# Causal attention on one core: no maximum pass, four row tiles for the scores, key sums on VectorE, a written order

## The chip, the core and the metric

The kernel runs on one core of a Trainium2 chip. The metric is the device time of one execution in microseconds, here written us. The core has five engines that work side by side, each through its own instructions in order: TensorE (PE in the profile; its weight loads are PEld), VectorE (DVE), ScalarE (ACT), GpSimd (POOL) and SyncE (SP), which only issues transfers here. All data are float32.

## The reference, cut to what matters

```python
# x: (32, 256, 32, 32), standard normal; q_w (256, 256), kv_w (512, 256) scaled by 1/16
xf = gn(x).reshape(B, C, S)                 # 32 groups of 8 channels; S = 1024
q = einsum('oc,bcs->bos', q_w, xf) + q_b
kv = einsum('oc,bcs->bos', kv_w, xf) + kv_b
k, v = kv[:, :256], kv[:, 256:]             # 8 heads of 32 channels
mask = tril(ones((S, S)), -1)               # a query sees earlier keys only, not itself
scores = where(mask == 0, -10000.0, q @ k.T / sqrt(32))
attn = where(mask == 0, 0.0, softmax(scores, axis=-1))
return x + attn @ v
```

Query 0 sees no key, so its attention is zero and its output is x. For every other query a hidden key adds exp(-10000 - largest) to the sum, which counts only where the largest visible score is near -10000.

## The kernel before, in words

The 256 channels lie on partitions in two chunks `g` of 128, four heads in each. Each of the 32 batches goes through two phases, and the first phase of a batch is interleaved with the second phase of the one before it.

The first phase normalises (`norm_channels`, `norm_mean`, `norm_apply`, L157 to L193), projects Q and K with channels on partitions (`project_qk`, L202, copied out by ScalarE at L206) and V with keys on partitions (`project_v`, L227, bias added by VectorE at L232). The maximum pass is `largest` (L247): for each block of 128 queries and each head a score product with queries on partitions, whose row maximum VectorE takes (L252, and L255 for the block with the diagonal). A head has 32 rows, so a product uses 32 of the 128 rows of the array. `shift_rows` (L268 to L282) turns the maxima into rows by a transpose and moves them by DMA into a 33rd row beside Q. For this, Q and K are also copied by DMA (L216) into tiles where the heads of a pair start at partitions 0 and 64.

The second phase takes, for each chunk, each half `hf` of 512 queries and each block `k` of 128 keys that the half sees, a step: `weights` computes the scores again with keys on partitions (L305), with 33 rows, two heads at a time; VectorE adds the mask to diagonal blocks (L311), ScalarE takes the exponential of two heads at once (L313). `values` (L332) multiplies the exponentials with V, four heads in four column tiles of 32, and a second time with a matrix of ones, which gives each query's sum of exponentials, copied to the 32 partitions of its head. `pick` (L323) starts the sums with what the hidden keys add. After the last key block ScalarE copies the accumulator out (L341), VectorE takes the reciprocal of 512 columns (L342) and multiplies (L343), GpSimd adds x (L348) and SP issues the output (L350).

A batch has 24 steps: per chunk four for the first half (512, 384, 256 and 128 queries see the key block) and eight for the second (five of 512, then 384, 256, 128). The order is that in which the program is written, one step behind for `values`, with the units of the next batch's first phase dealt out evenly over the steps (L369 to L387); the scheduler may still exchange instructions of an engine where dependencies allow it.

```python
for n in range(2):                       # values: V, then ones
    for j in range(4):
        jj, par = divmod(j, 2)
        nc.tensor.matmul(
            acc[HD * j : HD * (j + 1), n, c0:],
            lhsT=ones if n else live["v", b][:, k, h * HD : (h + 1) * HD],
            rhs=tiles[jj][:, par, c0:], ...)
```

Of the kernel before, what the change touches and what calls it, by code (L numbers as in the profile page):

```python
# [9 lines left out]
F32 = mybir.dt.float32  # L10
# [3 lines left out]
AX = mybir.AxisListType  # L14
PSUM = bass.MemoryType.PSUM
# [6 lines left out]
LOWEST = -1.0e30  # L22


@with_exitstack
def tile_norm_attention_residual(
# [25 lines left out]
    NB = S // P  # L52
    SCALE = 1.0 / math.sqrt(HD)

    const = ctx.enter_context(tc.tile_pool(name="const", bufs=1))
    xpool = ctx.enter_context(tc.tile_pool(name="xpool", bufs=3))
    npool = ctx.enter_context(tc.tile_pool(name="npool", bufs=2))
    apool = ctx.enter_context(tc.tile_pool(name="apool", bufs=3))
    vpool = ctx.enter_context(tc.tile_pool(name="vpool", bufs=2))
    epool = ctx.enter_context(tc.tile_pool(name="epool", bufs=6))  # L60
    opool = ctx.enter_context(tc.tile_pool(name="opool", bufs=2))
    small = ctx.enter_context(tc.tile_pool(name="small", bufs=3))
    ps_a = ctx.enter_context(tc.tile_pool(name="ps_a", bufs=2, space=PSUM))
    ps_s = ctx.enter_context(tc.tile_pool(name="ps_s", bufs=2, space=PSUM))
    ps_o = ctx.enter_context(tc.tile_pool(name="ps_o", bufs=1, space=PSUM))

    def bank(name):
        return ps_a.tile([P, HALF], F32, tag="bank", name=name)

# [4 lines left out]
    ident = const.tile([P, P], F32, name="ident")  # L74
    make_identity(nc, ident)
    ones = const.tile([P, HD], F32, name="ones")
    nc.gpsimd.memset(ones, 1.0)
    masked_bias = const.tile([P, 1], F32, name="masked_bias")
    nc.gpsimd.memset(masked_bias, MASKED)
# [3 lines left out]
    # Added to scores whose last 128 columns are a diagonal block [query, key].  # L83
    mask = const.tile([P, HALF], F32, name="mask")
    nc.gpsimd.memset(mask, 0.0)
    nc.gpsimd.affine_select(
        out=mask[:, HALF - P :], in_=mask[:, HALF - P :], pattern=[[-1, P]],
        compare_op=ALU.is_gt, fill=LOWEST, base=0, channel_multiplier=1,
    )
    # The same for a pair of heads' diagonal blocks [key, query].  # L90
    mask_t = const.tile([P, 2, P], F32, name="mask_t")
    nc.gpsimd.memset(mask_t, 0.0)
    nc.gpsimd.affine_select(
        out=mask_t, in_=mask_t, pattern=[[0, 2], [1, P]],
        compare_op=ALU.is_gt, fill=LOWEST, base=0, channel_multiplier=-1,
    )
# [46 lines left out]
    for n in range(3):  # L143
        t = const.tile([P, 2, S], F32, name=f"k_pair_{n}")
        for par in range(2):
            nc.gpsimd.memset(t[64 * par + HD : 64 * par + HD + 1, :, :], 1.0)
# [267 lines left out]
```

## Time and profile before

| | |
|---|---|
| timed runs | 7592.06, 7596.24 (median), 7607.42 us |
| span of the profiled execution, first to last instruction | 7550.2 us |
| other time of the profiled execution | not given on the page |
| instructions | 67242 |
| PE / DVE / ACT / POOL busy | 94% / 39% / 20% / 3% |
| mean granted TensorE clock | 0.737 |
| DMA, share of 16 engines | 6.5% |

A busy share counts time in which at least one instruction of the engine runs. Matmuls are pipelined and their ends are modelled, so rows of one engine can overlap, and the time of a group of products is read from its start to the start of the next. A granted clock of 1.00 is 2.4 GHz, 0.50 is 1.2 GHz.

### The profile page before, as it was taken

The numbers are of one execution on the slowest core, as the hardware profiler recorded it, in microseconds if no ns is written. First come the engines' busy times: TensorE is split into PE (matmuls) and PEld (weight loads), VectorE is DVE, ScalarE is ACT, GpSimd is POOL, SyncE is SP. The second block draws the span as 40 slices with busy tenths as digits, with TensorE's granted clock in tenths as the row PEclk, the third lists the DMA queues.
The fourth block names the chain that finished last, engine by engine and source line by source line (L and its number), as shares of the span: only waits on it lengthen the run. The fifth ranks groups of instructions, "written<-read, shape, count | busy, mean of one in ns | idle before, by whom it ended". The sixth has DMA issues, their size and how long they took to land. (4 is left out here: it accounts for less than half of the span.)

```text
span 7550.2 us, 67242 instructions
## 1 busy us (share of the span) xinstructions
PE 7074.5 (94%) x27084; PEld 2446.2 (32%) x27084; DVE 2918.8 (39%) x7272; ACT 1512.2 (20%) x1985; POOL 199.6 (3%) x185
## 2 busy tenths in 40 slices
PE   8999999999999999999999999999999999999999
PEld 3333333333333333333333333333333333333333
DVE  4333333343343334333333333333343334334433
ACT  0111212112122122221211212121121211212213
POOL 0000000000000000000000000000000000000000
PEclk6767777777677768777777767777776777777778
DMA  1000000000000000000000000000000000000000
GB/s 35 13 23 15 23 11 21 23 15 23 9 23 23 15 23 19 13 23 15 23 15 17 23 15 23 9 23 23 15 23 11 21 23 15 23 19 14 23 12 15
DMA packets 50713, 141.59 MB, mean 19 GB/s; under 512 B 12640, under 2 KB 17632, under 8 KB 50400
## 3 DMA queue, kind: packets, MB, share of 16 engines
q1 hardware_dynamic: 50400, 137.28, 6.5%
q8 instruction: 213, 3.49, 0.2%
q14 instruction: 100, 0.82, 0.0%
HBM read 34.47 MB, written 33.55 MB: 9 GB/s over the span
## 5 line engine op out<-in xcount | busy, mean ns | idle before, releaser
L247 PE MATMUL sc<-k,q 32*128 32x512 f32 (+3 forms) x6144 | 2606.8, 719 | 419.6 <-DVE far L252 245.0
L313 ACT ACTIVATE e<-sT 128x1024 f32<-128x1024 f32 (+3 forms) x1536 | 1195.3, 809 | 5208.2 <-DVE sT L311 3900.3
L247 PEld LDWEIGHTS sc<-k,q 32*128 32x128 f32 x6144 | 902.2, 235 | 2262.4 <-DVE top L255 939.4
L305 PE MATMUL sT<-q_pair,k_pair 33*128 33x512 f32 (+3 forms) x6144 | 1588.9, 614 | 2.1 <-ACT e L313 0.8
L332 PE MATMUL acc<-e,v 128*32 128x512 f32 (+3 forms) x6144 | 1374.6, 664 | 0.0
L332 PE MATMUL acc<-e,ones 128*32 128x512 f32 (+3 forms) x6144 | 1355.5, 656 | 0.0
L305 PEld LDWEIGHTS sT<-q_pair,k_pair 33*128 33x128 f32 x6144 | 642.0, 225 | 1036.0 <-issue 933.7
L252 DVE TENSOR_REDUCE far<-sc 128x1 f32<-128x512 f32 x1024 | 680.4, 688 | 635.6 <-PE sc L247 635.6
L255 DVE CUSTOM_DVE_ANT_0 junk<-sc,mask,far 128x128 f32<-128x128 f32 (+3 forms) x1024 | 560.5, 550 | 918.5 <-PE sc L247 917.0
L255 DVE CUSTOM_DVE_ANT_0 junk<-sc,mask 128x128 f32<-128x128 f32 (+3 forms) x1024 | 473.2, 485 | 1104.8 <-PE sc L247 1104.6
L311 DVE TENSOR_TENSOR sT<-sT,mask_t 128x256 f32<-128x256 f32 x1024 | 430.1, 429 | 1125.4 <-PE sT L305 1005.4
L342 DVE RECIPROCAL acc_sb<-acc_sb 128x512 f32<-128x512 f32 x128 | 429.1, 3352 | 301.5 <-ACT acc_sb L341 301.5
L202 PE MATMUL pp<-xn,wT 128*128 128x512 f32 x1024 | 542.5, 679 | 1.0 <-DVE xn L190 1.0
L332 PEld LDWEIGHTS acc<-e,ones 128*32 128x32 f32 x6144 | 286.5, 135 | 465.0 <-issue 446.0
L332 PEld LDWEIGHTS acc<-e,v 128*32 128x32 f32 x6144 | 192.7, 122 | 746.8 <-issue 712.4
L348 POOL TENSOR_TENSOR y<-acc_sb,x 128x512 f32<-128x512 f32 x128 | 162.2, 1267 | 6758.2 <-DVE acc_sb L343 5663.0
L202 PEld LDWEIGHTS pp<-xn,wT 128*128 128x128 f32 x1024 | 213.3, 219 | 303.0 <-issue 267.4
L227 PE MATMUL ppv<-wT,xn 128*128 128x256 f32 x1024 | 242.5, 385 | 22.9 <-DVE v L232 22.9
L227 PEld LDWEIGHTS ppv<-wT,xn 128*128 128x128 f32 x1024 | 189.5, 190 | 75.6 <-DVE v L232 28.5
L255 DVE DVE_READ_ACCUMULATOR2_ANT top<- 128x1 f32 x2048 | 170.3, 83 | 0.0
L341 ACT COPY acc_sb<-acc 128x1024 f32<-128x1024 f32 x128 | 129.6, 1012 | 194.9 <-PE acc L332 194.8
L323 PE MATMUL acc<-extra,pick 4*128 4x512 f32 x256 | 168.4, 742 | 0.0
(50 smaller groups left out, 811.4 us busy)
## 6 DMA issues: line engine op xcount, KB each, us to landing
x<-in_x_dram SPq DMA_DIRECT2D x32, 1024.0 KB
q_pair<-q SPq DMA_DIRECT2D x256, 128.0 KB
k_pair<-k SPq DMA_DIRECT2D x256, 128.0 KB
out_dram<-y SPq DMA_DIRECT2D x64, 512.0 KB
q_pair<-rows SPq DMA_DIRECT2D x128, 8.0 KB
extra<-rows SPq DMA_DIRECT2D x64, 16.0 KB
wn<-in_L_conv_kv_w_dram SPq DMA_DIRECT2D x2, 256.0 KB
wn<-in_L_conv_q_w_dram SPq DMA_DIRECT2D x1, 256.0 KB
```

What stands on the lines that cost most here:

```text
L202: nc.tensor.matmul(pp, lhsT=wT[:, cc, n * C + g * P : n * C + (g + 1) * P], rhs=xn[:, cc, hf * HALF : (hf + 1) * HALF], start=cc == 0, sto ...
L227: nc.tensor.matmul(pp[:, s, :], lhsT=xn[:, cc, (2 * n + s) * P : (2 * n + s + 1) * P], rhs=wT[:, cc, 2 * C : 3 * C], start=cc == 0, stop=c ...
L247: nc.tensor.matmul(sc[:, : k1 - k0], lhsT=q[rows, i * P : (i + 1) * P], rhs=k[rows, k0:k1], start=True, stop=True,)
L252: nc.vector.tensor_reduce(far[:, r, i : i + 1], sc[:, : k1 - k0], AX.X, ALU.max)
L255: nc.vector.tensor_tensor_reduce(out=junk[:, : k1 - k0], in0=sc[:, : k1 - k0], in1=mask[:, HALF - (k1 - k0) :], scale=1.0, scalar=far[:, r ...
L305: nc.tensor.matmul(sc[:, par, c0:], lhsT=k2[rows, jj, k * P : (k + 1) * P], rhs=q2[rows, jj, hf * HALF + c0 : (hf + 1) * HALF], start=True ...
L311: nc.vector.tensor_add(diagonal, diagonal, mask_t)
L313: nc.scalar.activation(e[:, :, c0:], sc[:, :, c0:], AF.Exp)
L323: nc.tensor.matmul(live["acc"][:, 1, :], lhsT=pick, rhs=live["extra", b, g][:, hf * HALF : (hf + 1) * HALF], start=True, stop=False, skip_ ...
L332: nc.tensor.matmul(acc[HD * j : HD * (j + 1), n, c0:], lhsT=ones if n else live["v", b][:, k, h * HD : (h + 1) * HD], rhs=tiles[jj][:, par ...
L342: nc.vector.reciprocal(both[:, 1, :], both[:, 1, :])
L348: nc.gpsimd.tensor_add(y[:, cols], both[:, 0, :], live["x", b][:, g, cols])
```

## The change

The kernel gets two functions. `unshifted` computes everything with exponentials of the plain scores; it keeps track of whether every sum of exponentials lies within 1e-20 and 1e20. `shifted` computes everything with the maximum subtracted, in a loop over the batches, and stands behind a branch on that record.

In `unshifted` the maximum pass, `shift_rows`, the 33rd row, the DMA copies of Q and K and the products with ones are gone. A score step takes its four heads from partitions 0, 32, 64 and 96 of Q and K as projected, in four row tiles, into four banks. The diagonal block is masked after the exponential, by GpSimd. The sums of exponentials are first added over key blocks by VectorE (into the tile of the first key block), and only then over partitions by one product per head; the four (chunk, half) results of a batch share one tile `den`. Their reciprocal is taken once per batch in four pieces, spread to the heads' partitions by 16 DMAs, multiplied and added to x some steps into the next batch. `values` runs two steps behind `scores`. On PE, ACT, DVE and POOL the instructions stay in the order in which they are written.

PSUM before: 2 single banks, 2 pairs for scores, a pair as accumulator. After: 3 pairs for scores, 1 bank as accumulator, 1 bank for all else.

```diff
-            for par in range(2):
-                rows = slice(64 * par, 64 * par + HD + 1)
-                nc.tensor.matmul(
-                    sc[:, par, c0:], lhsT=k2[rows, jj, k * P : (k + 1) * P],
-                    rhs=q2[rows, jj, hf * HALF + c0 : (hf + 1) * HALF], start=True, stop=True,
-                )
-            if k * P >= hf * HALF:
-                diagonal = sc[:, :, c0 : c0 + P]
-                nc.vector.tensor_add(diagonal, diagonal, mask_t)
...
+        def scores(b, g, hf, k):
+            q, kk = live["q", b, g], live["k", b, g]
+            c0 = max(k * P - hf * HALF, 0)
+            tag = "e0" if k == 0 else "e"
+            e = epool.tile([P, 4, HALF], F32, tag=tag, bufs=2 if k == 0 else None, name=f"{tag}_{b}_{g}_{hf}_{k}")
+            pairs = [ps_s.tile([P, 2, HALF], F32, tag="sT", name=f"sT_{b}_{g}_{hf}_{k}_{a}") for a in range(2)]
+            for j in range(4):
+                rows = slice(HD * j, HD * (j + 1))
+                nc.tensor.matmul(
+                    pairs[j // 2][:, j % 2, c0:], lhsT=kk[rows, k * P : (k + 1) * P],
+                    rhs=q[rows, hf * HALF + c0 : (hf + 1) * HALF], start=True, stop=True,
+                )
+            for a in range(2):
+                nc.scalar.activation(e[:, 2 * a : 2 * a + 2, c0:], pairs[a][:, :, c0:], AF.Exp)
+            if k * P >= hf * HALF:
+                diagonal = e[:, :, c0 : c0 + P]
+                nc.gpsimd.affine_select(
+                    out=diagonal, in_=diagonal, pattern=[[0, 4], [1, P]],
+                    compare_op=ALU.is_gt, fill=0.0, base=0, channel_multiplier=-1,
+                )
+                if k == 0:
+                    nc.gpsimd.memset(e[0:1, :, 0:1], 1.0)
...
+        def values(b, g, hf, k):
...
+            for j in range(4):
+                h = 4 * g + j
+                nc.tensor.matmul(
+                    acc[HD * j : HD * (j + 1), c0:], lhsT=live["v", b][:, k, h * HD : (h + 1) * HD],
+                    rhs=e[:, j, c0:], start=k == 0, stop=k == last, skip_group_check=True,
+                )
+            if k:
+                nc.vector.tensor_add(total[:, :, c0:], total[:, :, c0:], e[:, :, c0:])
+            if k == last:
...
+                nc.scalar.copy(live["num", b][:, g, hf * HALF : (hf + 1) * HALF], acc)
+        def sums(b, g, hf):
+            n = NH * g + hf
+            total = live.pop(("sum", b, g, hf))
+            pd = misc(f"pd_{b}_{n}")
+            for j in range(4):
+                nc.tensor.matmul(
+                    pd[HD * j : HD * (j + 1), :], lhsT=pick[:, n, :], rhs=total[:, j, :],
+                    start=True, stop=True, skip_group_check=True,
+                )
+            if n == 0:
+                live["den", b] = small.tile([P, HALF], F32, tag="den", name=f"den_{b}")
+                nc.vector.tensor_copy(live["den", b], pd)
+            else:
+                nc.vector.tensor_add(live["den", b], live["den", b], pd)
+        def check_sums(b):
+            den = live["den", b]
+            nc.vector.scalar_tensor_tensor(in_range, den, SUM_MIN, in_range, ALU.is_ge, ALU.mult)
+            nc.vector.scalar_tensor_tensor(in_range, den, SUM_MAX, in_range, ALU.is_le, ALU.mult)
+        def invert(b, c):
...
+            cols = slice(c * P, (c + 1) * P)
+            nc.vector.reciprocal(live["rec", b][:, cols], live["den", b][:, cols])
+        def spread(b):
...
+                    nc.sync.dma_start(
+                        out=rb[HD * j : HD * (j + 1), n // NH, (n % NH) * HALF : (n % NH + 1) * HALF],
+                        in_=src.unsqueeze(1).broadcast_to([1, HD, HALF]),
+                    )
+        def finish(b, n):
...
+            nc.vector.tensor_mul(rb[:, g, cols], num[:, g, cols], rb[:, g, cols])
+            nc.gpsimd.tensor_add(rb[:, g, cols], rb[:, g, cols], xt[:, g, cols])
...
+        for b in range(B):
+            if b + 2 < B:
+                when(b * N, lambda b=b: load(b + 2))
+                for n, f in zip((4, 6, 10, 14, 16, 18), prepare(b + 2)):
+                    when(b * N + n, f)
+            if b + 1 < B:
+                for n, f in enumerate(projections(b + 1)):
+                    when(b * N + 2 * n + 1, f)
+            for s, (g, hf, k) in enumerate(per):
+                if k == (hf + 1) * BPH - 1:
+                    when(b * N + s + LAG + 2 + (s + LAG) % 2, lambda b=b, g=g, hf=hf: sums(b, g, hf))
+            end = (b + 1) * N + LAG + 2
+            when(end, lambda b=b: check_sums(b))
+            for c in range(BPH):
+                when(end + 1 + c, lambda b=b, c=c: invert(b, c))
+            when(end + BPH, lambda b=b: spread(b))
+            for n in range(4):
+                when(end + BPH + 5 + n, lambda b=b, n=n: finish(b, n))
+        with tc.manual_schedule(engines={ENG.PE, ENG.Activation, ENG.DVE, ENG.Pool}):
...
+            for i in range(max(max(at), len(steps) + LAG) + 1):
+                if i < len(steps):
+                    scores(*steps[i])
+                for f in at.get(i, ()):
+                    f()
+                if LAG <= i < len(steps) + LAG:
+                    values(*steps[i - LAG])
...
+    outside = unshifted()
+    again = nc.values_load(outside[0:1, 0:1], min_val=0, max_val=P)
+    with tc.If(again > 0):
+        shifted()
```

Here `N` is 24, `LAG` is 2, `NH` 2 and `BPH` 4. Twelve projection units of the next batch (four of Q and K, four of V, four of Q and K) stand at the odd steps.

## Rows read from the trace of the kernel before

**Rows 1.** Part 1 of the page: span, busy time and share, instructions of each engine.

```profile
span 7550.2 us, 67242 instructions
PE 7074.5 (94%) x27084; PEld 2446.2 (32%) x27084; DVE 2918.8 (39%) x7272; ACT 1512.2 (20%) x1985; POOL 199.6 (3%) x185
```

**Rows 2.** Part 5, cost groups: busy us, mean ns | idle before, what ended it.

```profile
L247 PE MATMUL sc<-k,q 32*128 32x512 f32 (+3 forms) x6144 | 2606.8, 719 | 419.6 <-DVE far L252 245.0
...
L332 PE MATMUL acc<-e,ones 128*32 128x512 f32 (+3 forms) x6144 | 1355.5, 656 | 0.0
...
L323 PE MATMUL acc<-extra,pick 4*128 4x512 f32 x256 | 168.4, 742 | 0.0
```

**Rows 3.** Mean clock; stretches: us, busy us (count) by engine, granted clock, DMA.

```profile
core 0: 7550.2 us, clock 0.737
...
7480.00:7515.00 35.00, 34.50 (x270) 11.82 (x262) 12.62 (x20) 16.21 (x22) 2.53 (x2) 1.00 0.04 16
...
3100.00:3120.00 20.00, 18.76 (x53) 6.23 (x50) 6.71 (x16) 1.79 (x3) 0.00 (x0) 0.50 0.00 0
```

**Rows 4.** Timeline, projections in a stretch at full clock: start us, us, instruction, count.

```profile
3254.35 3.70 PE L202 MATMUL pp<-xn,wT 128*128 128x512 f32 x8
...
3257.89 1.89 PE L227 MATMUL ppv<-wT,xn 128*128 128x256 f32 x8
...
3263.68 3.72 PE L227 MATMUL ppv<-wT,xn 128*128 128x256 f32 x16
```

**Rows 5.** Timeline of the last batch, PE, at full clock.

```profile
7484.11 1.04 PE L332 MATMUL acc<-e,ones 128*32 128x512 f32 x8
7485.09 1.99 PE L305 MATMUL sT<-q_pair,k_pair 33*128 33x512 f32 x8
7487.00 1.06 PE L332 MATMUL acc<-e,v 128*32 128x512 f32 x8
7487.89 1.04 PE L332 MATMUL acc<-e,ones 128*32 128x512 f32 x8
...
7497.71 0.83 PE L332 MATMUL acc<-e,ones 128*32 128x384 f32 x8
...
7498.47 0.71 PE L305 MATMUL sT<-q_pair,k_pair 33*128 33x128 f32 x8
...
7499.11 0.64 PE L332 MATMUL acc<-e,v 128*32 128x256 f32 x8
```

**Rows 6.** Groups by line and shape, DVE: busy us, mean ns.

```profile
L342 DVE RECIPROCAL acc_sb<-acc_sb 128x512 f32<-128x512 f32 x128 | 429.1, 3352 | 301.5 <-ACT acc_sb L341 301.5
...
L232 DVE TENSOR_TENSOR v<-ppv,v_bias 128x256 f32<-128x256 f32 x256 | 94.8, 412 | 79.8 <-PE ppv L227 79.8
...
L343 DVE TENSOR_TENSOR acc_sb<-acc_sb 128x512 f32<-128x512 f32 x128 | 87.5, 683 | 0.1
```

**Rows 7.** The same view, ACT.

```profile
L313 ACT ACTIVATE e<-sT 128x1024 f32<-128x1024 f32 x768 | 755.3, 1021 | 2546.3 <-PE sT L305 1296.9 <-DVE sT L311 1247.2
```

**Rows 8.** The same view, POOL.

```profile
L348 POOL TENSOR_TENSOR y<-acc_sb,x 128x512 f32<-128x512 f32 x128 | 162.2, 1267 | 6758.2 <-DVE acc_sb L343 5663.0 <-issue 1095.2
...
L93 POOL TENSOR_SCALAR_AFFINE_SELECT mask_t<-mask_t 128x256 f32<-128x256 f32 x1 | 0.4, 406 | 0.0
```

**Rows 9.** Timeline, one VectorE instruction twice: beside GpSimd, and alone.

```profile
3132.33 1.27 POOL L348 TENSOR_TENSOR y<-acc_sb,x 128x512 f32<-128x512 f32 x1 [94.08 <-DVE acc_sb L343]
...
3132.43 1.21 DVE L270 TENSOR_TENSOR both<-both,hidden 128x32 f32<-128x32 f32 x1
...
3240.08 0.19 DVE L270 TENSOR_TENSOR both<-both,hidden 128x32 f32<-128x32 f32 x1 [0.39 <-ACT both L269]
```

**Rows 10.** Timeline, SP's queue: four issues.

```profile
3015.21 3.37 SPq L216 DMA_DIRECT2D k_pair<-k  x4
```

**Rows 11.** Timeline, start of the program: the first projection.

```profile
24.83 9.02 PE L202 MATMUL pp<-xn,wT 128*128 128x512 f32 x16 [0.97 <-DVE xn L190]
```

More of the change, by code (lines that the diff above doesn't have):

```diff
@@ L22 @@
 LOWEST = -1.0e30
+SUM_MIN = 1.0e-20
+SUM_MAX = 1.0e20
+LAG = 2
 @with_exitstack
@@ L52, in tile_norm_attention_residual @@
     NB = S // P
+    NH = S // HALF
+    BPH = HALF // P
     SCALE = 1.0 / math.sqrt(HD)
     const = ctx.enter_context(tc.tile_pool(name="const", bufs=1))
[L56 to L68, printed above, removed]
     x_in = x.rearrange("b (g p) h w -> b p g (h w)", p=P)
@@ L214, in project_qk @@
-        for j in range(4):
-            jj, par = divmod(j, 2)
-            nc.sync.dma_start(out=pair[64 * par : 64 * par + HD, jj, :], in_=t[HD * j : HD * (j + 1), :])
-        live["qk"[n], b, g], live["qk"[n] + "2", b, g] = t, pair
-    def project_v(b, n):
-        xn = live["xn", b]
-        if n == 0:
-            live["v", b] = vpool.tile([P, NB, C], F32, tag="v", name=f"v_{b}")
-        pp = bank(f"ppv_{b}_{n}").rearrange("p (s c) -> p s c", c=C)
-        for s in range(2):
-            for cc in range(NG):
+                live[key][:, cols], pp, AF.Identity, bias=qk_bias[:, n, g : g + 1], scale=(SCALE, 1.0)[n],
+            )
@@ L317, in values @@
-    def values(b, g, hf, k, tiles):
-        last = (hf + 1) * (HALF // P) - 1
-        c0 = max(k * P - hf * HALF, 0)
-        if k == 0:
-            live["acc"] = ps_o.tile([P, 2, HALF], F32, tag="acc", name=f"acc_{b}_{g}_{hf}")
-            nc.tensor.matmul(
-                live["acc"][:, 1, :], lhsT=pick, rhs=live["extra", b, g][:, hf * HALF : (hf + 1) * HALF],
-                start=True, stop=False, skip_group_check=True,
-            )
-        acc = live["acc"]
-        for n in range(2):
+                    pairs[j // 2][:, j % 2, c0:], lhsT=kk[rows, k * P : (k + 1) * P],
@@ L332, in values @@
                 nc.tensor.matmul(
-                    acc[HD * j : HD * (j + 1), n, c0:],
-                    lhsT=ones if n else live["v", b][:, k, h * HD : (h + 1) * HD],
-                    rhs=tiles[jj][:, par, c0:], start=n == 0 and k == 0, stop=k == last,
-                    skip_group_check=True,
-                )
-        if k < last:
-            return
-        both = opool.tile([P, 2, HALF], F32, tag="both", name=f"acc_sb_{b}_{g}_{hf}")
-        nc.scalar.copy(both, acc)
-        nc.vector.reciprocal(both[:, 1, :], both[:, 1, :])
@@ new lines, in unshifted, with when, prepare @@
+        per = [(g, hf, k) for g in range(NG) for hf in range(NH) for k in range((hf + 1) * BPH)]
+        steps = [(b, *s) for b in range(B) for s in per]
+        N = len(per)
+        at = {}
+        def when(i, f):
+            at.setdefault(i, []).append(f)
+        def prepare(b):
+            return [
+                lambda: norm_channels(b, 0), lambda: norm_channels(b, 1), lambda: norm_mean(b),
+                lambda: norm_rstd(b), lambda: norm_apply(b, 0), lambda: norm_apply(b, 1),
+            ]
@@ new lines, in unshifted @@
+        with tc.manual_schedule(engines={ENG.PE, ENG.Activation, ENG.DVE, ENG.Pool}):
+            for b in range(min(2, B)):
+                load(b)
+                for f in prepare(b):
+                    f()
+            for f in projections(0):
+                f()
+            for i in range(max(max(at), len(steps) + LAG) + 1):
+                if i < len(steps):
+                    scores(*steps[i])
+                for f in at.get(i, ()):
+                    f()
+                if LAG <= i < len(steps) + LAG:
+                    values(*steps[i - LAG])
+            worst = const.tile([P, 1], F32, name="worst")
+            nc.vector.tensor_reduce(worst, in_range, AX.X, ALU.min)
+            pc = misc("pc")
+            nc.tensor.matmul(pc[0:1, 0:1], lhsT=worst, rhs=ones, start=True, stop=True)
+            outside = const.tile([1, 1], I32, name="outside")
+            nc.vector.tensor_scalar(outside, pc[0:1, 0:1], -1.0, float(P), ALU.mult, ALU.add)
```

414 lines of the change are left out of this document (218 added, 196 removed).

## The prediction

> **What bounds the kernel now.** I read the page's engine line first [rows 1]: TensorE is busy 94% of a span of 7550.2 us, VectorE 39%, ScalarE 20%, GpSimd 3%. So the time is TensorE's, and the next two questions are what it does and how fast. The page's cost groups [rows 2] answer the first: the score products of the maximum pass (L247) hold 2606.8 us of busy time and have 419.6 us of idle ahead of them, ended by VectorE, which reads one bank after another; the products with a matrix of ones (L332), which only add up the exponentials, hold 1355.5; the one with `pick` (L323) 168.4. These overlap with other products, so they are not to be subtracted from the span. The granted clock answers the second [rows 3]: 0.737 on average, between its two levels of 0.50 (1.2 GHz) and 1.00 (2.4 GHz). Where the maximum pass runs beside the rest (3100 to 3120) it is 0.50; in the last batch, where no maximum pass is left, it is 1.00 from 7480 to 7515, with TensorE busy 34.50 of 35 us. What the last batch does there is close to what the changed kernel does all the time, so its timeline gives the prices.
>
> **The change, part by part.** All prices are at 2.4 GHz, per batch, with 24 steps (two chunks of 4 and 8 key blocks): 12 steps of 512 queries, and four each of 384, 256 and 128.
>
> Scores. One 512-column instruction takes 0.44 us (eight of them one behind the other, 3254.35 to 3257.89) [rows 4], and a float32 product is two of them. In the last batch eight score instructions of 512 run from 7485.09 to 7487.00, 1.91 us [rows 5]: four slots of 0.43, two heads in each, and 0.2 for the change of tile shape. With four row tiles I take two slots and the same 0.2: 1.06. At 128 columns the row is 0.64 (7498.47 to 7499.11), so 0.43 with four (two slots of 0.11 and the 0.2). Between them on a line: 0.85 and 0.64. Sum: 12 x 1.06 + 4 x (0.85 + 0.64 + 0.43) = 20.4. Four row tiles at once are in no row. The bounds are the 0.89 in which four column tiles do the same columns (7487.00 to 7487.89) and the 1.91 of two pairs; I take 1.06 since the column tiles reach all four.
>
> Values. Their ones products go, 1355.5 us of busy time [rows 2]. What is left costs as the ones rows, with the change of shape behind them: 0.98 at 512, 0.75 at 384 (7497.71 to 7498.47) [rows 5], on the same line 0.54 and 0.33. Sum: 12 x 0.98 + 4 x 1.62 = 18.2.
>
> Projections stay: eight units of Q and K at 1.77 (3.54 for two) and four of V at 1.86 (3.72 for two) [rows 4] make 21.6. New are the column sums of the key sums through `pick`, four times 0.98, 3.9. The two small products of the norm I put at 0.8, like two of the narrowest above. **TensorE: 64.9 us per batch**, 32 batches 2077.
>
> VectorE loses the maximum pass and the mask, and gains the key sums: `total` plus `e`, four heads wide, for all but the first key block. From 683 ns at 512 columns and 412 at 256 [rows 6] a column costs 1.06 ns and an instruction 0.14 us more: 2.31 us at four times 512, then 1.77, 1.23 and 0.68. Eight of the first and four of each other: 33.2. The rest is worked at the same price: statistics and normalised x 5.5, V's bias 2.7 (four of 512), sums into `den` 2.7, two checks 1.4, four reciprocals of 128 columns 3.4 (a quarter of 3352 ns each), the last products 2.7: 18.4. **VectorE: 51.6 per batch**, below TensorE. It isn't below it everywhere: in steps 4 to 11, where wide key blocks meet statistics, checks and reciprocals, I count 24.1 for VectorE and 23.2 for TensorE.
>
> ScalarE keeps its exponentials, 1021 ns for a pair of 512 [rows 7], and copies half as much out of the accumulator. It was 1512.2 us in all [rows 1] and does not grow: at most 47.3 per batch, hidden behind TensorE. But a full step without projections has 2.04 of each (TensorE 1.06 + 0.98, ScalarE 2 x 1.02), so there it is no faster; the projections in every second step pay that back.
>
> GpSimd gets the causal mask: 16 selections of 512 elements per batch. 128 x 256 took 406 ns [rows 8]; doubled, less what is fixed, some 0.63, so 10.1; four last additions at 1267 ns [rows 8] 5.1. With small ones about 16. New waits hang on it: a value product and VectorE's key sum come behind the selection, and behind a late value product stand the scores of the next step, since the order is fixed. Two steps (5.4 us on average) lie between scores and values, against two exponentials (2.04) and a selection: hidden, as long as the selection starts promptly.
>
> It may not. A row of 32 columns on VectorE with two inputs in SBUF took 0.19 us alone and 1.21 us when a GpSimd addition of 1.27 had begun 0.1 us earlier [rows 9]: it waited for it. The key sums have two SBUF inputs too. Per batch 33.2 + 1.4 + 2.7 of such work and 16 of GpSimd's could so take turns: VectorE then ends between 53 and 68 us instead of 51.6.
>
> Queues. SP loses 704 issues (q_pair, k_pair, rows, extra) and gets 512 (16 per batch, in `spread`). Four took 3.37 us [rows 10], so 16 take 13.5. The first product of `finish` on VectorE waits for the thirteenth, 11 us and a landing; five steps (13 us) lie between: 0 to 3 us per batch, and behind a waiting VectorE stand the key sums and then the `e` buffers. I take it as hidden.
>
> One accumulator bank and one miscellaneous bank replace larger pools. The copy out of the accumulator ends about 0.3 us after the next group wants it, four times a batch.
>
> How much of this shows? If the queues carry everything over, a batch is TensorE's 64.9. If nothing carries from one step to the next, it is the sum over the steps of the largest of TensorE, VectorE with GpSimd, and ScalarE, by these prices 79.4 (72.0 without the turns with GpSimd). Most is lost at step 4 (VectorE 4.9 against 2.6), at 8 and 10 (3.8 and 2.9 against 3.0 and 2.0) and at 14 to 16. The two steps of lag carry most: I take a third of the way, 69.7. 32 x 69.7 = 2230.
>
> Ends. The first projection began at 24.83 [rows 11]; twelve units on one bank with ScalarE reading in between cost some 11 more than their 21.6, which stand in the sum already: 36. The end has a chain with nothing beside it: a sum 0.98, `den` and checks 2, reciprocals 3.4, 16 issues 13.5, a last product and addition 2, landings and the check's result: 24 by rows, 30 with the landings as an estimate (bounds 24 to 50). The skipped branch is in it; no row shows one.
>
> **Sum**: 2230 + 36 + 30 = 2296 of span. The page gives the profiled execution's span and no other time for it; the median of the runs, 7596.24, lies 46.0 above it. With the same 46: **2342**, say 2345 us.
>
> **The rivals.** (1) *Turns with GpSimd and steps without carry.* By [rows 9] every selection stops the key sums or waits for one. At 79.4 per batch: 2541 + 66 + 46 = 2653. For it: the 1.21 us row. Against: lag of two steps, and VectorE's own slack of 13 us. Chance 0.13, from 2500 up.
> (2) *The four row tiles don't run at once*, the part that would not do what it says: heads go in pairs as now. Scores cost 1.91 and so on, 15.4 more per batch, TensorE 80.3, VectorE hidden: 32 x 82 + 112 = 2740. For it: only pairs are seen. Against: column tiles run by fours. Chance 0.08. Half way, a score row of about 1.5, adds 0.43 x 18 = 7.7 per batch, of which the stalls above take back some 2: 2345 + 180 = 2525, chance 0.06.
> The Trainium skill, page "TensorE: Matmul & The Clock Gate", section "Measured speedup vs the span model", gives 3.07 times for four row tiles of 32 rows and 512 columns, not 4. By that figure the sum would be some 150 us longer than mine (an estimate from the page); no row here decides it.
> (3) *The clock doesn't hold.* A batch has 128 slots of 512 columns (36 each for scores and values, 48 for projections, 8 for sums); at 0.43 they are 55.0 of the 64.9. At the mean of now, 0.737, they take 74.6, with the other 9.9 that is 84.5: 2704 + 112 = 2816. For it: the maximum pass's rows show that it falls where TensorE works on few rows and waits. Against: 1.00 in the last batch [rows 3], in work like this. Chance 0.08.
> (4) *The branch is taken* (slower). If a sum of exponentials lies outside 1e-20 to 1e20, everything is computed again in the loop of `shifted`. That has 64 rounds a batch; each has on VectorE on average 4.5 copies, a reduction and several more, no less than 3 us by the prices of [rows 6]: 2048 x 3 = 6100 on top, over 8400 us in all. The point is a score near 46 (the logarithm of 1e20). Scores here are products of normalised channels with weights of 1/16 over 32 channels, of about unit spread. Chance 0.02.
> (5) Faster still, everything carried: 64.9 x 32 + 112 = 2189. It is the low end of the forecast.
>
> **How the numbers follow.** The forecast, TensorE bound at full clock with part of the stalls, has 0.62; another 0.01 is for what I haven't thought of. Predicted is its time, 2345. The low end of the range is everything carried, 2185; the high end takes in (1), the half way case and (2), 2750; (3) and (4) stay outside. About 0.2% (15 us) is what a measurement can tell from no change. Cases slower than before have 0.02, none lies near it (0.01), so faster has 0.97.
>
> **What would show it.** Right: TensorE busy over 90% with the clock near 1.00; score rows of 512 from start to next start about 1.06; VectorE near 1650 us busy, GpSimd near 520; no instruction of `shifted`. Wrong: score rows at 1.9 (rival 2); key sums much longer than 2.31 us or selections of 2 us, with TensorE waiting for the selection (rival 1); a clock under 0.9 (rival 3); TensorE idle ahead of projections, waiting for the single bank, which I priced at nearly nothing.

## The result and the profile after

| | before | after |
|---|---|---|
| median, four runs each | 7594.15 us (7528.08 to 7607.42) | 2988.11 us (2987.26 to 2990.66) |
| ratio after / before | | 0.3941, 95% interval 0.3926 to 0.3957 |
| profiled execution / its span | | 2987.61 / 2985.9 us |
| PE / DVE / ACT / POOL busy | 94% / 39% / 20% / 3% | 78% / 56% / 46% / 32% |
| mean granted clock | 0.737 | 0.886 |

The kernel is 2.5 times as fast, but the time lies 643 us above the forecast of 2345 and outside its range of 2185 to 2750. None of the rivals describes it: TensorE works at the prices of the sum and stands still for the rest. The page says so in a few lines: engines and clock, the DMA queue that moved nearly all bytes, the chain that ended last, two groups with the idle time ahead of them, and the issues.

```profile
PE 2317.2 (78%) x15502; PEld 860.3 (29%) x15502; DVE 1671.4 (56%) x1641; ACT 1386.7 (46%) x1921; POOL 960.5 (32%) x817
...
PEclk9988898888998888998889988889988889888885
...
q1 hardware_dynamic: 44000, 101.62, 40.7%
...
PE 47%; SPq 23%; DVE 13%; DMA 12%; issue 3%; ACT 1%; POOL 0%; DVEq 0%; POOLq 0%
...
L297 DVE TENSOR_TENSOR rb<-num,rb 128x512 f32<-128x512 f32 x128 | 90.4, 707 | 689.7 <-DMA rb<-rec 689.7
...
L153 PE MATMUL pv<-dev,avg 128*128 128x2 f32 x64 | 18.6, 360 | 532.5 <-DVE v L196 530.9
...
rb<-rec SPq DMA_DIRECT2D x512, 64.0 KB, 10.7
```

Against [rows 1], TensorE is no longer the whole story: 22% of the span is without it. The chain goes through SP's queue for 23% and through transfers for 12%, which together is over a third of the span on the path. The L297 row is the largest single wait: VectorE stood 689.7 us, 21.6 per batch, ahead of the first products of `finish`, until the DMA of `spread` had landed. The L153 row is its echo on TensorE, which stands behind VectorE.

How one becomes the other is seen in the timeline of one batch, here SP and VectorE:

```profile
1516.92 31.52 SPq L287 DMA_DIRECT2D rb<-rec  x16
...
1527.15 0.68 DVE L196 TENSOR_TENSOR v<-ppv,v_bias 128x512 f32<-128x512 f32 x1
1527.75 3.08 DVE L248 TENSOR_TENSOR e<-e,e 128x1536 f32<-128x1536 f32 x2
1549.93 0.69 DVE L297 TENSOR_TENSOR rb<-num,rb 128x512 f32<-128x512 f32 x1 [19.10 <-DMA rb<-rec]
1550.54 0.68 DVE L196 TENSOR_TENSOR v<-ppv,v_bias 128x512 f32<-128x512 f32 x1
```

and in three stretches of it (columns: PE, PEld, DVE, ACT, POOL busy, granted clock, share of the DMA engines, GB/s):

```profile
1516.90:1533.30 16.40, 16.37 (x130) 7.82 (x122) 12.31 (x12) 8.79 (x13) 7.75 (x7) 1.00 0.84 27
1533.30:1550.00 16.70, 0.00 (x0) 0.00 (x0) 0.07 (x1) 1.09 (x2) 0.00 (x0) 0.56 0.91 31
1550.00:1603.00 53.00, 51.38 (x335) 17.72 (x336) 35.64 (x36) 30.98 (x43) 21.44 (x18) 0.95 0.17 43
```

Sixteen issues take 31.5 us, 1.97 each on average (the shortest of all issues 0.51, the median 2.36), and the first product needs the thirteenth transfer, the fourth head's first: 1516.92 + 12 x 1.97 + 10.7 to land is 1551, the row says 1549.93. VectorE reaches that product at 1530.8 and waits 19.10. Behind it in VectorE's queue stands the bias of V, which empties the one miscellaneous bank; the next product in TensorE's order (L153) needs that bank, and TensorE is idle for 16.70 of 16.70 us. The DMA engines are 0.91 busy in that stretch and move 31 GB/s. The granted clock, 1.00 while TensorE had work, is 0.56 on average in the stretch without, and 0.95 in what follows.

### The profile page after: what moved, and what is told of

It is laid out like the page before. It is cut to its first block, busy times and chain, and to the rows that moved or that the text cites. A ratio compares the mean times of both kernels' runs of the same rounds, so it can differ in the third digit from the quotient of the medians.

```text
span 2985.9 us, 38251 instructions
## 1 busy us (share of the span) xinstructions
PE 2317.2 (78%) x15502; PEld 860.3 (29%) x15502; DVE 1671.4 (56%) x1641; ACT 1386.7 (46%) x1921; POOL 960.5 (32%) x817
## 4 chain that ended last, share of the span: by engine, by line
PE 47%; SPq 23%; DVE 13%; DMA 12%; issue 3%; ACT 1%; POOL 0%; DVEq 0%; POOLq 0%
SPq L287 23%; PE sT L215 14%; PE pp L176 13%; PE acc L243 12%; DMA rb<-rec 12%; DVE e L248 4%; PE ppv L191 4%; PE pd L260 3%; DVE rec L279 3%; DVE st L135 2%; DVE v L196 1%; DVE in_range L272 1%; DVE den L268 1%; DVE in_range L273 1%; PE pv L153 1%
## 5 line engine op out<-in xcount | busy, mean ns | idle before, releaser
L248 DVE TENSOR_TENSOR e<-e,e 128x2048 f32<-128x2048 f32 (+3 forms) x640 | 1126.5, 1760 | 242.9 <-PE acc L243 147.2
L225 POOL TENSOR_SCALAR_AFFINE_SELECT e<-e 128x512 f32<-128x512 f32 x512 | 714.8, 1405 | 1293.1 <-ACT e L220 1287.9
L215 PE MATMUL sT<-q,k 32*128 32x512 f32 (+3 forms) x6144 | 821.6, 541 | 0.5 <-ACT e L220 0.5
L243 PE MATMUL acc<-e,v 128*32 128x512 f32 (+3 forms) x6144 | 679.0, 515 | 19.2 <-ACT num L252 11.3
L297 DVE TENSOR_TENSOR rb<-num,rb 128x512 f32<-128x512 f32 x128 | 90.4, 707 | 689.7 <-DMA rb<-rec 689.7
L215 PEld LDWEIGHTS sT<-q,k 32*128 32x128 f32 x6144 | 294.5, 188 | 557.2 <-issue 301.8
L153 PE MATMUL pv<-dev,avg 128*128 128x2 f32 x64 | 18.6, 360 | 532.5 <-DVE v L196 530.9
L298 POOL TENSOR_TENSOR rb<-rb,x 128x512 f32<-128x512 f32 x128 | 178.8, 1397 | 694.4 <-DVE rb L297 693.8
L153 PEld LDWEIGHTS pv<-dev,avg 128*128 128x128 f32 x64 | 15.8, 307 | 544.7 <-DVE v L196 542.8
L260 PE MATMUL pd<-e,pick 128*32 128x512 f32 x1024 | 138.1, 612 | 19.8 <-DVE e L248 19.8
L180 ACT ACTIVATE k<-pp,qk_bias 128x512 f32<-128x512 f32 x128 | 88.2, 689 | 76.5 <-PE pp L176 74.2
L279 DVE RECIPROCAL rec<-den 128x128 f32<-128x128 f32 x128 | 118.6, 930 | 0.0
## 6 DMA issues: line engine op xcount, KB each, us to landing
rb<-rec SPq DMA_DIRECT2D x512, 64.0 KB, 10.7
```

Source lines behind the costliest of these rows:

```text
L180: nc.scalar.activation(live[key][:, cols], pp, AF.Identity, bias=qk_bias[:, n, g : g + 1], scale=(SCALE, 1.0)[n],)
L215: nc.tensor.matmul(pairs[j // 2][:, j % 2, c0:], lhsT=kk[rows, k * P : (k + 1) * P], rhs=q[rows, hf * HALF + c0 : (hf + 1) * HALF], start= ...
L225: nc.gpsimd.affine_select(out=diagonal, in_=diagonal, pattern=[[0, 4], [1, P]], compare_op=ALU.is_gt, fill=0.0, base=0, channel_multiplier=-1,
L243: nc.tensor.matmul(acc[HD * j : HD * (j + 1), c0:], lhsT=live["v", b][:, k, h * HD : (h + 1) * HD], rhs=e[:, j, c0:], start=k == 0, stop=k ...
L248: nc.vector.tensor_add(total[:, :, c0:], total[:, :, c0:], e[:, :, c0:])
L260: nc.tensor.matmul(pd[HD * j : HD * (j + 1), :], lhsT=pick[:, n, :], rhs=total[:, j, :], start=True, stop=True, skip_group_check=True,)
```

## The experiments

Ten kernels, in three groups on three chips: e1 to e4, e5 to e8, and e9 with e10. The kernel before took 7592.05, 7606.41 and 7588.51 us there, so a difference of some 0.3% (7 us) between kernels of different groups says nothing by itself. e1 and e3 were timed twice, e5 four times, the others once.

| | time, us | span | clock | 16 (or 4) spread issues, us | VectorE's wait for the spread, us |
|---|---|---|---|---|---|
| after | 2988.11 | 2985.9 | 0.886 | 31.5 | 689.7 |
| e1_late_finish | 2375.25 | 2374.1 | 0.985 | 31.6 | 37.2 |
| e2_heads_inside | 2463.35 | 2461.4 | 0.969 | 20.9 | 146.7 |
| e3_eight_rows | 2343.09 | 2341.4 | 0.993 | 11.6 | 10.8 |
| e4_no_spread | 2327.76 | 2326.1 | 0.995 | none | none |
| e5_four_transfers | 2334.32 | 2332.5 | 0.995 | 2.5 | 2.4 |
| e6_no_selection | 2318.38 | 2316.6 | 0.993 | as e3 | 10.8 |
| e7_before_no_maximum | 3435.56 | 3433.9 | 0.952 | | |
| e8_other_sources | 2689.22 | 2687.5 | 0.923 | 22.5 | 332.6 |
| e9_lag_one | 2348.02 | 2346.3 | 0.992 | as e5 | 2.4 |
| e10_scheduler_order | 2816.05 | 2814.3 | 0.920 | as e5 | 88.7 |

### Is it the wait alone? `finish` later: e1_late_finish

```diff
-                when(end + BPH + 5 + n, lambda b=b, n=n: finish(b, n))
+                when(end + BPH + 14 + n, lambda b=b, n=n: finish(b, n))
```

> The transfers of the spread stay as they are; the four finish units run nine steps later (some 25 us). Theory A (VectorE waits for rb, and everything behind it stands): the 689.7 us of VectorE's wait go, 2300 to 2400 us, granted clock near 0.98. Rival B (the wait only shows where another limit, the turns of VectorE and GpSimd, would hold the kernel anyway): the time stays above 2800 us and the key sums or the selections take over the wait.

2375.25 us, ratio to before 0.3127 (0.309 to 0.316). The transfers are as slow as they were (10.6 us to land, 16 issues in 31.6), only nobody waits for them, except in the last batch (36.6 of the 37.2 us):

```profile
L297 DVE TENSOR_TENSOR rb<-num,rb 128x512 f32<-128x512 f32 x128 | 161.1, 1259 | 37.2 <-DMA rb<-rec 37.2
...
1217.90 31.59 SPq L287 DMA_DIRECT2D rb<-rec  x16
...
1288.71 1.78 SPq L287 DMA_DIRECT2D rb<-rec  x3
```

From spread to spread a batch takes 70.8 us (1217.90 to 1288.71), as long as with the quick transfers of e3 below. So within the batches the slowness costs time by VectorE's wait and by nothing else; the traffic itself takes nothing from the engines. The 32 us that e1 lies above e3 are mostly the wait at the end.

### What makes the issues slow? e2_heads_inside, e8_other_sources, e3_eight_rows

In the changed kernel each transfer reads one row (one partition) 32 times, and four in a row read neighbouring rows of one head. The second kernel exchanges the loops, so that consecutive transfers go to another head's rows and partitions:

```diff
-            for j in range(4):
-                for n in range(4):
+            for n in range(4):
+                for j in range(4):
```

> Same 16 transfers, other order: the four heads of one (chunk, half) follow each other, so that transfers next to each other read from partitions 32 apart instead of from neighbours. Theory A1 (the transfers are slow because each reads one row 32 times, and neighbours read through the same place): they overlap, the 31.5 us of the 16 issues fall, and the time falls to between 2350 and 2700 us. Rival A2 (every transfer costs SP some 2 us whatever it reads): 31.5 us and 2986 us as before. The Trainium skill, page SBUF - State Buffer, section Door 1: the DMA port swizzle, puts partitions that differ by 32 on one port and those that differ by 64 on two; by that rule the issues would halve, to some 16 us.

The third leaves the destinations in order and changes the source rows alone:

```diff
-                    src = rec[HD * j + n : HD * j + n + 1, :]
+                    r = HD * ((j + n) % 4) + n
+                    src = rec[r : r + 1, :]
```

> The changed kernel, with one row a source and the destinations in their order, but the four transfers of a head read rows 32 partitions apart (so rows go to the wrong heads). If it is the neighbouring source rows that hold each other up, 16 issues take about 21 us, as with the heads inside, and the kernel 2440 to 2500 us. If it is the neighbouring destinations, they take 31.5 us as in the changed kernel, and it takes 2960 to 3010.

The fourth uses that `pick` puts a sum on eight rows of a head already (every fourth), and reads all eight, each four times:

```diff
-                    src = rec[HD * j + n : HD * j + n + 1, :]
+                    src = rec[HD * j + n : HD * (j + 1) : 4, :]
...
-                        in_=src.unsqueeze(1).broadcast_to([1, HD, HALF]),
+                        in_=src.unsqueeze(1).broadcast_to([HD // 4, 4, HALF]),
```

> Same 16 transfers of 64 KB in the same order, but each reads eight rows of rec (all hold the same sums) four times each, instead of one row 32 times. Theory A1 (one source row is the limit): issues fall below 1 us each, 16 of them to 8 to 14 us, VectorE's wait for rb below 100 us in all, 2300 to 2420 us. Rival A2 (a fixed cost per transfer): 1.97 us each and 2986 us as before.

The timelines of SP, one spread of each, e2, e8 and e3:

```profile
1495.57 20.85 SPq L287 DMA_DIRECT2D rb<-rec  x16
```

```profile
1457.95 22.52 SPq L288 DMA_DIRECT2D rb<-rec  x16
```

```profile
1003.55 11.59 SPq L287 DMA_DIRECT2D rb<-rec  x16
```

The same 1 MB over the same number of issues takes 31.5, 20.9, 22.5 and 11.6 us. Sources that lie 32 partitions apart bring most of the gain that heads inside brought (22.5 against 20.9), with the destinations unmoved: it is the reading side. And with eight source rows per transfer an issue takes 0.68 us, near the 0.84 of four plain copies [rows 10]. What is slow is reading the same row, and rows beside it, over and over: 64 KB in 1.97 us is 33 GB/s.

Part 3 of the pages tells whether it is the issuing or the moving that is slow. These are the queue's lines of e2, e8, e3 and e4, which has no spread:

```profile
q1 hardware_dynamic: 44000, 101.62, 32.8%
...
q1 hardware_dynamic: 44000, 101.62, 32.3%
...
q1 hardware_dynamic: 39904, 101.61, 11.8%
...
q1 hardware_dynamic: 19424, 68.03, 8.0%
```

The share times the span times 16 engines, less the same of e4, is the time that the spread's 16384 rows of 2 KB spent on the DMA engines. By this estimate a row took 1.0 us in the changed kernel, 0.67 in e8, 0.61 in e2 and 0.09 in e3. The 512 rows of a batch on 16 engines then need 32, 21, 19 and 3 us. In the first three that is about what the 16 issues take, so the moving sets the pace and SP is held behind it; in e3 the issues themselves are what is left. (e3 also has 40 packets per transfer instead of 48, which no run separates from the number of rows.)

The time of e8 was missed. I expected 2440 to 2500 because its issues are as quick as e2's; it took 2689.22. What I left out is the order: the first product needs all four heads of the first (chunk, half), which are the first four transfers in e2 and the first, fifth, ninth and thirteenth in e8. Its wait is 332.6 us against 146.7:

```profile
L298 DVE TENSOR_TENSOR rb<-num,rb 128x512 f32<-128x512 f32 x128 | 100.4, 787 | 332.7 <-DMA rb<-rec 332.6
```

e3 takes 2343.09 us (2343.05 to 2343.12), ratio 0.3085 (0.3053 to 0.3117). Only the last batch still waits for the spread:

```profile
PE 2238.4 (96%) x15502; PEld 822.5 (35%) x15502; DVE 1735.8 (74%) x1641; ACT 1386.4 (59%) x1921; POOL 1002.1 (43%) x817
...
L297 DVE TENSOR_TENSOR rb<-num,rb 128x512 f32<-128x512 f32 x128 | 146.0, 1144 | 10.9 <-DMA rb<-rec 10.8
```

### Without the spread: e4_no_spread

It leaves out the 16 transfers; `finish` multiplies with the reciprocals as they lie.

```diff
-            nc.vector.tensor_mul(rb[:, g, cols], num[:, g, cols], rb[:, g, cols])
+            nc.vector.tensor_mul(rb[:, g, cols], num[:, g, cols], live["rec_used", b])
```

> Leaves out the spread: finish multiplies by rec as it lies, so the output is not the reference's. It shows what the kernel costs with no transfer to wait for. Theory A: 2290 to 2380 us, clock 0.97 or more; at 69.7 us per batch by the prediction's sum it would be 2298. Rival B: above 2800 us.

2327.76 us. This is what the spread can give back at most; e3 lies 15.3 above it, most of that in the 11.6 us of issues at the end, where nothing lies beside them.

### Fewer transfers: e5_four_transfers

Since a row p of `rec[n::4]` belongs to head p // 8 and goes to partitions 4p to 4p + 3, the heads need no transfers of their own:

```diff
-            for j in range(4):
-                for n in range(4):
-                    src = rec[HD * j + n : HD * j + n + 1, :]
...
+            for n in range(4):
+                src = rec[n::4, :]
+                nc.sync.dma_start(
+                    out=rb[:, n // NH, (n % NH) * HALF : (n % NH + 1) * HALF],
+                    in_=src.unsqueeze(1).broadcast_to([HD, 4, HALF]),
+                )
```

> The spread as four transfers a batch instead of 16: each reads 32 rows of the reciprocals and writes each of them to four partitions. If the spread costs by its issues (0.68 us each with eight rows a source) and by rows read over and over, four issues take 2.7 us, no wait is left behind them but that of the last batch, and the end gets some 6 to 9 us shorter: 2333 to 2341 us. If a transfer of 256 KB lands much later than one of 64 KB, the first product waits again in every batch: 2360 to 2450.

2334.32 us (2333.91 to 2337.15), ratio 0.3067 (0.3053 to 0.308). Four issues take 2.5 us, and a transfer lands 2.5 us after its issue. In the last batch:

```profile
2318.52 2.48 SPq L286 DMA_DIRECT2D rb<-rec  x4
2320.93 3.62 DVE L296 TENSOR_TENSOR rb<-num,rb 128x512 f32<-128x512 f32 x4 [2.44 <-DMA rb<-rec]
```

The wait of 10.82 at the end has become 2.44, and the kernel is 8.8 us shorter than e3: both as expected. (The two ran on different chips; what shows the gain is the end in the traces.) It is the fastest of the kernels that do all of the work, 654 us below the changed one.

### Do VectorE and GpSimd take turns? e6_no_selection

The diff takes the `affine_select` of `scores` out of e3.

> On the kernel with eight rows a source; it leaves out the causal selection on GpSimd within the diagonal blocks. If the turns of selections and key sums cost the time nothing, since TensorE waits for a selection only some 9 us in all there: 2325 to 2350. If the turns are what separates a batch of 70.8 us from TensorE's 64.9, as my first rival has it: 2160 to 2260. In both cases the key sums of 512 columns should fall from 2.34 us towards the 2.23 they take alone.

2318.38 us, 24.7 (1.1%) below e3 in a single run on another chip: under 1 us per batch, a little more than my first figure allowed and far from the second. The cost groups by form tell what the turns do to the engines, e5 (with selections) first, then e6:

```profile
L248 DVE TENSOR_TENSOR e<-e,e 128x2048 f32<-128x2048 f32 x256 | 599.8, 2343 | 59.4 <-ACT e L220 52.4
L248 DVE TENSOR_TENSOR e<-e,e 128x1536 f32<-128x1536 f32 x128 | 253.1, 1978 | 150.7 <-PE acc L243 146.9 <-DVE e L248 0.5
L248 DVE TENSOR_TENSOR e<-e,e 128x1024 f32<-128x1024 f32 x128 | 178.4, 1393 | 6.7
...
L248 DVE TENSOR_TENSOR e<-e,e 128x512 f32<-128x512 f32 x128 | 105.5, 824 | 6.8
...
L225 POOL TENSOR_SCALAR_AFFINE_SELECT e<-e 128x512 f32<-128x512 f32 x512 | 705.6, 1387 | 1282.3 <-ACT e L220 1282.3
```

```profile
L243 DVE TENSOR_TENSOR e<-e,e 128x2048 f32<-128x2048 f32 x256 | 583.7, 2280 | 74.6 <-ACT e L220 67.7
L243 DVE TENSOR_TENSOR e<-e,e 128x1536 f32<-128x1536 f32 x128 | 230.8, 1803 | 182.9 <-PE acc L238 156.7 <-ACT e L220 17.1 <-PE sT L215 5.6
L243 DVE TENSOR_TENSOR e<-e,e 128x1024 f32<-128x1024 f32 x128 | 170.2, 1330 | 6.7
...
L243 DVE TENSOR_TENSOR e<-e,e 128x512 f32<-128x512 f32 x128 | 86.3, 674 | 7.1 <-DVE e L243 0.5
```

VectorE's widest additions take 3% longer beside selections, the narrowest 22%, all of them together 66 us more (1136.7 against 1070.9). The selections give way most: 1.39 us on average in e5, where the shortest takes 0.63; times 512 that is some 390 us.

```profile
L225 POOL TENSOR_SCALAR_AFFINE_SELECT e<-e x512: 627/951/2681, 63.7 to 2307.0; 128x512 f32<-128x512 f32 x171
```

That the additions are the reason can be read in e5's trace: the 129 selections that overlap no addition take 0.68 us on average, the 258 that lie for over 60% of their time beside one take 2.06. Both engines have the slack for it: VectorE is busy 74% of the span, GpSimd 43%.

### What did the maximum pass cost? e7_before_no_maximum

```diff
-            units += [lambda i=i, jj=jj, g=g: largest(b, g, i, jj) for i in range(NB) for jj in range(2)]
...
-        top = live.pop(("top", b, g))
+        top = small.tile([P, 4, NB], F32, tag="top", name=f"top_{b}_{g}")
+        nc.gpsimd.memset(top, 0.0)
...
-    nc.gpsimd.memset(masked_bias, MASKED)
+    nc.gpsimd.memset(masked_bias, -30.0)
```

> The kernel before without its maximum pass: the maxima are set to 0 and the hidden keys' part to a small constant, so no score product of the maximum pass runs and VectorE has no row maxima; all else is as before (pairs of heads, products with ones, 33rd row). If the loss of the clock was the maximum pass's doing, TensorE has some 96 us a batch at full clock (scores 36, values and ones 37, projections 22, the rest 1 to 2): 3150 to 3400 at a granted clock over 0.95. If the clock stays near 0.74, 3900 to 4300.

3435.56 us, 36 above the upper end of what I gave, at a clock of 0.952.

```profile
PE 3331.6 (97%) x20940; PEld 1279.4 (37%) x20940; DVE 1213.3 (35%) x2152; ACT 1488.5 (43%) x1985; POOL 207.1 (6%) x249
```

So the kernel before gets 4171 us shorter (its runs here: 7606.41) by leaving out this pass alone, row maxima on VectorE included, more than the 3026.4 us that its products hold in busy and idle time [rows 2]: what remains also runs at 0.952 instead of 0.737 of the clock. The rest of the change (four row tiles, no products with ones, no 33rd row, key sums on VectorE, the mask on GpSimd, the written order), not taken apart here, brings 3436 down to 2343 in e3; the spread as written gives 645 of that back.

### Lag and order: e9_lag_one, e10_scheduler_order

Both on e5. The first has

```diff
-LAG = 2
+LAG = 1
```

> On the kernel with four transfers a batch: the products with V run one step behind the scores instead of two. If the second step of lag is what carries work over from one step to the next, as my sum has it (a third of the way from 64.9 to 79.4 us a batch), one step carries hardly any: TensorE waits for exponentials and selections in most steps, 79 us a batch or more, 2560 to 2800 us. If one step is enough cover, 2330 to 2400.

2348.02 us, 13.7 (0.6%) more in one run on another chip, within my second range and far below the first. My idea of the lag falls: one step covers nearly everything. (`LAG` also stands in the schedule, so column sums, spread and `finish` come about a step earlier too.) The products with V wait more for selections, 49.4 us in all, where e5 has 7.9:

```profile
L243 PE MATMUL acc<-e,v 128*32 128x512 f32 (+3 forms) x6144 | 654.7, 498 | 50.7 <-POOL e L225 49.4 <-POOL e L230 0.9 <-ACT num L252 0.3
```

The second leaves the order to the scheduler:

```diff
-        with tc.manual_schedule(engines={ENG.PE, ENG.Activation, ENG.DVE, ENG.Pool}):
+        with ExitStack():
```

> On the kernel with four transfers a batch: the order of PE, ACT, DVE and POOL is no longer fixed as written; the scheduler may exchange instructions of an engine. If the written order is what keeps TensorE fed, more waits and 2400 to 2700 us. If the scheduler keeps about the order in which the program is written, 2320 to 2360.

2816.05 us, 482 more than e5 and 116 above the upper end of my first range. The numbers of instructions on the four engines are the same; TensorE's largest new wait is ahead of V's projection, which needs the miscellaneous bank:

```profile
L191 PE MATMUL ppv<-wT,xn 128*128 128x256 f32 x1024 | 307.9, 452 | 376.0 <-DVE den L266 376.0
```

The timeline of one batch shows why the copy of `den` is late:

```profile
1461.92 6.75 DVE L248 TENSOR_TENSOR e<-e,e 128x2048 f32<-128x2048 f32 x2
...
1466.95 0.43 SPq L128 DMA_DIRECT2D x<-in_x_dram  x1
...
1472.40 1.29 DVE L135 BATCH_NORM_STATS2 st<-x 128x6 f32<-128x512 f32 x2 [3.72 <-DMA x<-in_x_dram]
1473.60 0.68 DVE L266 COPY den<-pd 128x512 f32<-128x512 f32 x1
1474.19 2.28 DVE L248 TENSOR_TENSOR e<-e,e 128x2048 f32<-128x2048 f32 x1
1474.33 3.51 PE L191 MATMUL ppv<-wT,xn 128*128 128x256 f32 x8 [12.55 <-DVE den L266]
```

The product that fills the bank begins at 1459.00 and takes 1.07 us. Between it and the copy VectorE's queue holds a last product of `finish`, two additions and the statistics of a batch that is still being loaded. In e5 these statistics stand ahead of the copy too, but there their load was issued 34 us before them (1384.11 and 1417.98), and here 5.5 us (1466.95 and 1472.40). It resembles the wait of the changed kernel: the emptying of the bank stands behind other things in VectorE's queue, and TensorE stands behind that. A transfer is only part of it here: while TensorE waited 12.55 us, VectorE worked 6.75 us on the additions, waited 3.72 for the DMA and worked 1.29 on the statistics. (It is one batch's reading. In the whole run TensorE is idle for 401 us more than in e5 and busy for 81 more, at a mean clock of 0.920; which exchanges cost how much was not taken apart.)

## Why the prediction was wrong

**The step that failed** is the one on queues: "0 to 3 us per batch ... I take it as hidden". It took an issue of the spread at 0.84 us, from four copies of K [rows 10], and the landing as short. Those copies read 32 partitions each; a spread transfer reads one partition 32 times, and in this kernel that is 1.97 us an issue on average and 10.7 us to land. The thirteenth transfer so lands 33 us after the first issue instead of 11 and a short landing. The distance was right: the first product was reached 13.9 us after the first issue, where 13 were counted. TensorE had work for 16.4 of the 33 us and none for the other 16.7 in the batch shown; per batch the kernel lost 19.3 us where the step had 0 to 3. A consequence stood in the step ("behind a waiting VectorE stand the key sums and then the `e` buffers"), though it was the single miscellaneous bank that stopped TensorE, a wait that the prediction had "priced at nearly nothing" and, ahead of projections, listed as a sign of being wrong. The price of the transfers was taken from the nearest row without a bound on the other side. I had no rival in which a transfer sets the time, so the range didn't reach it either.

How much it is: with the same work and eight source rows, e3 needs 2343.09, so the step is worth 645 us, where 643 were missed. A batch takes 90.1 us after (1516.92 to 1606.99, spread to spread) and 70.8 in e3. From the first spread to the last it is 2783 us (153.7 to 2937.08) against 2165 (153.9 to 2318.90), 618 more. At the end the last spread has nothing beside it: its issues take 31.95 us instead of 11.59, where the prediction had 13.5, and from its start to the end of the span it is 48.8 us instead of 22.5, 26 more. The sum is 645.

**The terms that held** are read in e3, from start to next start on TensorE over one batch, with the clock at 1.00:

```profile
1003.55:1074.37 70.82, 69.66 (x491) 25.58 (x487) 54.09 (x51) 43.28 (x61) 31.12 (x25) 1.00 0.13 45
```

| per batch, us | predicted | e3 |
|---|---|---|
| scores | 20.4 | 25.0, of it 20.6 at 1.07, 0.85, 0.65, 0.43 and 4.4 of waits |
| values | 18.2 | 18.7 |
| projections | 21.6 | 23.0 (1.91 and 1.92 instead of 1.77 and 1.86) |
| column sums | 3.9 | 3.5 |
| norm | 0.8 | 0.6 |
| carry | 4.8 | in the scores' 4.4 |
| sum | 69.7 | 70.8 |

- *Four row tiles at once* (rival 2): right, and already in the changed kernel. A full step's scores run from start to next start in 1.07 us, 1502.56 to 1503.63:

```profile
1501.78 0.85 PE L243 MATMUL acc<-e,v 128*32 128x384 f32 x8
1502.56 1.14 PE L215 MATMUL sT<-q,k 32*128 32x512 f32 x8
1503.63 1.07 PE L260 MATMUL pd<-e,pick 128*32 128x512 f32 x8
```

  Four products one after the other would be 4 x 0.88 by [rows 4], so this is 3.3 times as fast, with the change of tile shape in it. The 3.07 times of the Trainium skill ("TensorE: Matmul & The Clock Gate", "Measured speedup vs the span model") would make 1.15 of it, an estimate from the page against the 1.07 measured. The 150 us that I worked out from it come out only if 0.2 for the change of shape is added once more, and they are not in the rows.
- *Turns of VectorE and GpSimd* (rival 1): the turns are there, more on GpSimd's side, and cost some 25 us in all (e6). GpSimd's own term was mis-sized by them: 16 us per batch were forecast, near 520 in all, and it is busy 1002.1 in e3 (31.3 per batch), 706.4 of it in selections. It costs little because GpSimd has the time.
- *The clock* (rival 3): it was low, 0.886, but as a consequence. Among the kernels that differ only in the spread or in when it is read, it is the lower, the longer the wait: 0.886, 0.923 (e8), 0.969 (e2), 0.985 (e1), 0.993 (e3).
- *The branch* (rival 4): no instruction of `shifted` ran.
- *Carry*: the size was right, the reason only half. Seven of the 24 score rows of the batch last longer than the others of their shape. Six of them follow a step without a projection and wait mostly for the exponentials of that step (113.3 us in e3 for TensorE's weight loads, 3.5 per batch); this is the step where the prediction had ScalarE need as long as TensorE. The seventh holds a wait of 0.34 for the accumulator, and the longest one a projection's wait of 0.82 for the single bank. That the second step of lag carries the work over is refuted by e9.
- *Around the span*: I added 46 us, the difference between the median of the runs and the one profiled span. The executions of this study lie 1.7 us above their own spans (2987.61 and 2985.9; for the kernel before, 7563.34 and 7561.6). The 46 was a difference between two executions. In e3 this error is hidden by others: its batches are 1.1 longer, some 36 us, and its ends 75 us instead of 66. That e3 comes within 2 us of 2345 is luck to that extent. (The parts that the prediction lists for the end add up to 21.9, not the 24 it names; the 2 us decide nothing.)

## What to carry to other kernels

In these runs a transfer that copies one SBUF row to many partitions was not priced by its bytes: count the different rows that it and its neighbours read, and put the source on several partitions first if an engine can do it for nothing, as `pick` here does. A wait for a DMA in the middle of an engine's written order costs what stands behind it in the queue: here one product of 0.69 us stopped the emptying of the only miscellaneous bank, and so TensorE. Place the first reader of a transfer by issue time of the transfer it really needs plus landing, or order the transfers by who is read first.

## What had not been expected of the hardware

- 16 transfers of 64 KB within SBUF took 31.5 us where each read one row 32 times and neighbours read neighbouring rows, 20.9 and 22.5 where successive sources lay 32 partitions apart, and 11.6 where each read eight rows four times; four of 256 KB with 32 rows each took 2.5 us to issue and 2.5 to land. The Trainium skill ("SBUF — State Buffer", "Door 1: The DMA port swizzle (why `[64,N]` ≈ `[32,N]`)") has the speed of a transfer depend on how many ports its partitions reach, with partitions 0 to 3 and 32 to 35 on one port and 64 to 67 on another. If this is taken over the transfers that follow each other, the changed kernel reads through one port at a time, e2 and e8 through two, e3 through eight. The order of the times agrees; the halving to some 16 us that I estimated from it for two ports was not seen, and no run here shows the ports themselves.
- A selection of 128 x 512 on GpSimd took 0.68 us on average where it met none of VectorE's additions (0.63 at the least), 2.06 where it lay mostly beside one, and 1.39 over all, while an addition of 2048 columns was 2.28 without selections and 2.34 with them. The Trainium skill ("GPSIMD Engine Reference", "Key points") says that GpSimd shares its SBUF interfaces with VectorE and contends with VectorE instructions that have two SBUF inputs, which agrees. That the selections lose more than the additions is what these rows add; it is no rule, since in [rows 9] it was VectorE's instruction that grew from 0.19 to 1.21.
- The granted clock was 0.56 on average in the 16.7 us in which TensorE stood still in the batch shown, and 0.95 in the 53 us that followed. The waits so cost more than their own length, but little: TensorE was busy 2317.2 us after and 2238.4 in e3, 79 us more for the same products at a mean clock of 0.886 instead of 0.993.
